# A selective-scan, attention and FFN kernel: two directions' state projection in one TensorE operation, attention sums from the rows' own product, GpSimd adds ahead of the means

## The chip, the cores and the metric

One core of a Trainium2 chip computes the whole batch in one launch. The metric is the device time of that launch in microseconds (us); lower is better. The engines are TensorE (PE in the profile, with its weight loads listed apart as PEld), VectorE (DVE), ScalarE (ACT), GpSimd (POOL) and SyncE (SP). SP issues the DMAs of this kernel, in order.

## What is computed

The input is 8 images of 96 channels by 64 x 64 pixels (4096 positions), in float32. Layer 0 adds a state-space block to the image, layer 1 adds linear attention and then a quantised FFN:

```python
x = x + ssm(group_norm(x))
t = tokens(x)                            # (8, 4096, 96)
t = t + attn(layer_norm(t)); t = t + ffn(layer_norm(t))

def ssm(x):
    xi, z = split(layer_norm(x) @ in_proj_w.T + in_proj_b)      # 192 channels each
    xi = silu(depthwise_conv3x3(xi) + conv_b)
    xs = 4 directions: rows, columns, and both reversed         # k = 0, 1, 2, 3
    dts, Bs, Cs = split(x_proj_w[k] @ xs[k], [6, 16, 16])       # the state projection
    delta = softplus(dt_proj_w[k] @ dts + dt_proj_b)
    h = exp(delta * A) * h + delta * u * Bs;  y = sum_n(h * Cs) + D * u   # scan, 4096 steps
    y = sum of the four directions, turned back to rows
    return (layer_norm(y) * silu(z)) @ out_proj_w.T + out_proj_b

def attn(x):                             # no softmax: linear in the sums of k and v
    q, k, v = split(x @ Wqkv + bqkv)     # 6 heads of 16
    return ((q @ k.T) * 16**-0.5 @ v) @ Wff + bff     # per head
```

## The kernel before

Images go in pairs; four pairs. The program is nine stages in a row: an opening stage that prepares pair 0, then scan of pair 0, then a mixed stage that finishes pair 0 and prepares pair 1, scan of pair 1, and so on; after the fourth scan a last stage only finishes pair 3. Four scans, three mixed stages, an opening and a last stage. Between the stages all operands pass through DRAM tensors: zs (gate), us (scan input), dl (the step sizes, split in three bf16 parts), du (step size times input), bs and cs (states), ys (scan results), t1 and tn (tokens before and after normalisation).

A scan (function `scan`) is written out in order, by hand. The other stages are not: each operation is handed to a planner, class `Plan`, with an engine, a cost in us, what it reads and writes, the buffers that it takes from a ring, and a rank. `Plan.run` then plays the stage forward by those costs and emits the operations in the order in which they would start. Of the operations of an engine that could start within 0.1 us of the earliest, the one of lowest rank goes first; a DMA is costed by its size at 0.23 MB/us. That order is fixed when the program is built, and each engine and SP work through theirs strictly in turn. An operation whose index is in `claims` and which lacks buffers keeps operations of worse rank from taking buffers of that ring. A `unit` ring ("unit", "set", "turn", "chunk") limits how many groups of operations are in flight.

What the stages consist of, with the ranks that order them (constants at the top of the file):

- `project`: group norm, layer norm and input projection, chunk by chunk (512 positions, 8 chunks, 2 images); ranks up to FRONT.
- `convolve`: nine taps, on DVE for two thirds of the channels (L540) and as 32 x 32 matmuls for the rest (L552), in two halves; ranks FRONT to CONV.
- `prepare`: for o = 0 (rows, k = 0 and 2) and o = 1 (columns, k = 1 and 3), for each chunk c: `states` (L637), the state projection, per direction k; an ACT copy of its bank `pt` to `S`; DMAs of B and C; `steps_` (L657), six small matmuls that make the step sizes; then per third T of the channels softplus, products and splits on ACT and DVE (L670, L682, L686), and stores of du and dl. For o = 1 POOL first turns u (L624). Ranks PREP (0.08) to 1. The channels of two images lie in three tiles of 128 partitions: image 0, image 1, and 64 + 64 remaining ones. `xw` holds the projection's weights, three slabs per direction.
- `back`: for each of 16 blocks (chunk and image): loads of yk (from ys), ut, z3, xr; yd adds on DVE and POOL (L984); transposes on PE that gather the directions (L998); the skip term (L1010); the mean over 192 channels as two accumulating matmuls (`both`, L1017, with the matrix j192), its subtraction (L1022), squares on ACT, their mean by `both` again, Ln and Exp for the root (`root`), norm and gate (L1030, L1033), output projection (`both` with woT), residual (L1038) and layer norm (`norm`, L407 to L415). Then attention: `keys` (L1050) multiplies the tokens by the weights of K and V, 128 tokens at a time, ACT copies to `kv`, and `outer` (L1057) sums K^T V over all tokens in a bank `pm` of its own. Ranks 0 to BACK. At the end K^T V becomes one 97 x 96 matrix per image, hm (L1070 to L1079).
- `tail`: for the 16 blocks again, once hm is there: tn and t1 loads, tokens times hm (L1107), residual, norm, the FFN in fp8 (L1115 to L1132), the last add on POOL (L1134) and the store. Ranks TAIL to TAIL_END.

PSUM has a ring `q` of five banks, which nearly all matmuls share, a ring `hold`, and pm. Every activation goes through line 296, every planned DMA through line 315.

## Time and profile before

| | us |
|---|---|
| median of 3 runs (10145.36 to 10156.27) | 10145.48 |
| profiled execution | 10155.55 |
| its span, first to last instruction | 10153.8 |
| opening stage, 0 to 529 | 529.1 |
| scans | 1781.0, 1782.6, 1780.8, 1777.9 |
| mixed stages | 717.9, 719.1, 719.6 |
| last stage | 345.8 |

Stage bounds are the first scan instruction on DVE (L855) of each scan and the end of its last. Over the span DVE is busy 90%, POOL 74%, PE and DMA's main queue 71% and 78%, ACT 69%; the granted TensorE clock is 0.88 on average. A share over the span mixes scans with the other stages, so a stage is read by itself, from windows. In a window PE busy counts the matmuls (weight loads overlap them and stand apart), DMA share is that of the core's 16 DMA engines, and it can exceed 1.

### The profile page before, as it was taken

What the parts mean: (1) busy time and instruction counts of PE and PEld (TensorE: products, weight loads), DVE (VectorE), ACT (ScalarE), POOL (GpSimd) and SP (SyncE); (2) the same over time, 40 slices, a digit from 0 to 9 for tenths busy, and PEclk for the clock granted to TensorE, in tenths of its full rate; (3) what the DMA queues carried; (4) which work ended last, traced back from release to release, by engine and by line L of the source; (5) the groups of instructions that cost most, each with busy time, mean ns of one, the idle gap of its engine ahead of it and who ended that gap; (6) DMA issues with size and microseconds to landing.
All of it is one profiled execution on the core that took longest, in us unless ns stands there. A gap on an engine that the chain in (4) does not pass through costs nothing. (4 is left out here: it accounts for less than half of the span.)

```text
span 10153.8 us, 382989 instructions
## 1 busy us (share of the span) xinstructions
PE 7238.0 (71%) x166080; PEld 5184.5 (51%) x166080; DVE 9133.4 (90%) x7072; ACT 7028.9 (69%) x12289; POOL 7542.1 (74%) x2416
## 2 busy tenths in 40 slices
PE   6666676667876667666886666666688666676678
PEld 2155565554425556555442555555543355565554
DVE  7699999997679999999778999999877899999985
ACT  5667777776777777776677777777667777777754
POOL 2099999991039999999104999999810599999971
PEclk7689989998878998988887999998888799988989
DMA  4988888886988888887698888878769788788884
GB/s 132 235 211 215 214 215 213 214 213 138 241 216 213 214 214 216 213 214 188 165 243 211 211 215 213 217 212 214 191 167 240 208 213 216 212 216 214 213 193 102
DMA packets 1593915, 2085.10 MB, mean 205 GB/s; under 512 B 409891, under 2 KB 1050404, under 8 KB 1588644
## 3 DMA queue, kind: packets, MB, share of 16 engines
q1 hardware_dynamic: 1592228, 2060.59, 78.3%
q8 instruction: 1304, 21.36, 1.0%
q14 instruction: 383, 3.14, 0.1%
HBM read 1601.99 MB, written 458.04 MB: 203 GB/s over the span
## 5 line engine op out<-in xcount | busy, mean ns | idle before, releaser
L855 DVE TENSOR_TENSOR_SCAN h<-da,dbu 128x774 f32<-128x774 f32 x4096 | 7025.9, 1759 | 139.5 <-POOL dbu L819 43.5
L819 POOL TENSOR_TENSOR dbu<-dut,bc 128x1536 f32<-128x1536 f32 x2048 | 7083.4, 3575 | 73.6 <-DMA dm<-dl 30.2
L844 ACT ACTIVATE da<-da 128x768 f32<-128x768 f32 x4092 | 3260.2, 797 | 1984.4 <-PE da L837 1968.0
L837 PE MATMUL da<-dm,aw 128*128 128x128 bf16 x24576 | 2279.9, 235 | 2268.3 <-DVE h L855 2078.8
L837 PEld LDWEIGHTS <-aw 128*128 128x128 bf16 x24576 | 1792.8, 104 | 2512.4 <-issue 2233.3
L873 PE MATMUL yp<-h,cw 128*32 128x48 f32 x131072 | 2904.7, 238 | 101.7 <-issue 88.3
L873 PEld LDWEIGHTS yp<-h,cw 128*32 128x32 f32 x131072 | 2412.1, 154 | 548.4 <-issue 228.3
L773 ACT ACTIVATE cw<-bc,blk 128x512 f32<-128x512 f32 x2048 | 1472.4, 720 | 74.3 <-DMA dut<-du 36.0
L984 POOL TENSOR_TENSOR yd<-yk 128x768 f32<-128x768 f32 x64 | 126.7, 1981 | 918.3 <-DMA yk<-ys 630.4
L1134 POOL TENSOR_TENSOR yk<-yk,yd 96x512 f32<-96x512 f32 x64 | 100.1, 1565 | 775.7 <-issue 406.0
L624 POOL COPY A<-A 128x512 f32<-128x512 f32 x96 | 135.7, 1423 | 676.6 <-ACT A L296 375.2
L881 ACT ACTIVATE yev<-yp 128x384 f32<-128x384 f32 x1024 | 505.4, 494 | 81.6 <-PE yp L873 81.3
L296 ACT ACTIVATE A<-A 128x512 bf16<-128x512 bf16 (+1 forms) x777 | 445.8, 618 | 145.1 <-DMA dl<-A 108.6
L816 ACT COPY dbu<-h 128x12 f32<-128x12 f32 x1984 | 409.2, 206 | 0.0
L682 DVE TENSOR_TENSOR A<-A 128x512 f32<-128x512 f32 x384 | 287.2, 751 | 88.6 <-ACT A L296 87.2
L657 PE MATMUL q<-A 6*64 6x512 f32 x1536 | 301.0, 734 | 78.7 <-ACT A L296 65.5
L686 DVE TENSOR_TENSOR A<-A 128x512 bf16<-128x512 f32 x384 | 279.8, 729 | 83.8 <-DMA dl<-A 81.6
L540 DVE SCALAR_TENSOR_TENSOR A<-A,c_convw,A 128x2048 f32<-128x2048 f32 x128 | 299.2, 2363 | 0.6
L998 PEld LDWEIGHTS q<-ident,yd 128*96 128x96 f32 x2048 | 248.1, 169 | 82.9 <-issue 62.2
L998 PE MATMUL q<-ident,yd 128*96 128x128 f32 x2048 | 260.9, 281 | 15.4 <-DVE yd L984 9.3
L296 ACT ACTIVATE A<-q,c_dtb 128x512 f32<-128x512 f32 x384 | 253.7, 677 | 7.0 <-PE q L657 6.0
L411 PE MATMUL q<-small,c_j 96*96 96x512 f32 x384 | 230.1, 693 | 28.8 <-ACT small L296 19.1
(125 smaller groups left out, 5271.8 us busy)
## 6 DMA issues: line engine op xcount, KB each, us to landing
dut<-du SPq DMA_DIRECT2D x2048, 384.0 KB
dm<-dl SPq DMA_DIRECT2D x1024, 288.0 KB
dl<-A SPq DMA_DIRECT2D x256, 384.0 KB
dm<-dl SPq DMA_DIRECT2D x1024, 96.0 KB
ys<-yev SPq DMA_DIRECT2D x1024, 96.0 KB
du<-A SPq DMA_DIRECT2D x256, 256.0 KB
bc<-cs SPq DMA_DIRECT2D x512, 128.0 KB
bc<-bs SPq DMA_DIRECT2D x512, 128.0 KB
```

What stands on the lines that cost most here:

```text
L296: "ACT", cost, lambda: nc.scalar.activation(dst(), src_(), func, **kw),
L540: dve(P, 2.34, lambda o=o, v=v, w=w: nc.vector.scalar_tensor_tensor(o, v, w, o, ALU.mult, ALU.add), (), wr, (), first + (CONV - FRONT) / 2 ...
L657: nc.tensor.matmul(P[pqs[T]][o : o + 64], dtw[at : at + RK, k, o : o + 64], P[S][at : at + RK], start=True, stop=True,)
L773: nc.scalar.activation(cw[i % 2][:, :, :, m, :].rearrange("p z j t -> p (z j) t"), bc[i][:, 1].rearrange("p z (j t) -> p (z j) t", j=NB), ...
L816: nc.scalar.copy(start, segs(hs[s - 1][:, :, r])[:, :, :, 1 if back else TC])
L819: nc.gpsimd.tensor_tensor(segs(t)[:, :, :, 1:], dut[g].unsqueeze(1) .to_broadcast([128, 2, NI, TC]), bc[s // NB][:, 0, :, bass.ts(c % NB, ...
L837: nc.tensor.matmul(e[:, i], aw[k, r][:, i, z, :], dm[s // 2][:, NI * r + i, bass.ts(c % 2, TC)], start=True, stop=True,)
L844: nc.scalar.activation(e, e, AF.Exp)
L855: nc.vector.tensor_tensor_scan(hs[s][:, w, r][:, d], da[p % 3][:, o : o + W6][:, d], dbu[4 * s + r][:, w][:, d], 0.0, ALU.mult, ALU.add,)
L873: nc.tensor.matmul(y[32 * q : 32 * q + 32, 2 * NE * i : 2 * NE * i + 2 * NE] .rearrange("p (j r i) -> p i j r", j=2, r=NR), w[:, z, :, t], ...
L881: nc.scalar.activation(yev[s][:, :, o : o + 8, :].rearrange("p j i e -> p i j e"), y[:, 0 : 16 * NE].rearrange("p (i j e) -> p i j e", j=2 ...
L998: nc.tensor.matmul(o, P[yd][:, k, j, DIM * g : DIM * g + DIM], ident, start=(k + j == 0), stop=(k + j == 4),)
```

## The change

The five ranks at the top change: projection and convolution take later ranks, the back blocks earlier ones, the tail ranks behind all of `prepare`.

`states` becomes one operation for the two directions k = o and k = o + 2. For k >= 2 the halves of image 0 and image 1 are swapped (`xw`, `S`, `dtw` and the DMAs of B and C follow), so that the products of the third tile, which are cut from 128 rows (half of them zeros) to the 64 rows that matter, are four 64 x 64 tiles in four quarters of the array. It takes two q banks at once and claims them. S becomes three deep; dtw is loaded in eight pieces instead of four.

Ahead of each of the two means POOL adds the two halves of 96 channels into a buffer of the ring `small` (now six deep in mixed stages), and the mean is one matmul.

`keys` gives way to `rows`: a transpose of the tokens (with the identity, 97 columns with the constant 1), one ACT copy of four blocks, and `outer` sums the 97 x 97 product of the tokens with themselves. After the last block that matrix is multiplied by the weights of K and of V, two more matmuls and copies per image.

```diff
-FRONT = 0.05
-CONV = 0.35
+FRONT = 0.2
+CONV = 0.5
-BACK = 0.7
-TAIL = 0.66
-TAIL_END = 1.29
+BACK = 0.39
+TAIL = 1.04
+TAIL_END = 1.25
...
-                    o = 64 * b + 32 * g
+                    o = 64 * (b ^ (k // 2)) + 32 * g
...
-            dma(P, 0.03, lambda at=at, o=o, n=n: dtw[at : at + RK, :, o : o + n],
-                lambda r=r, T=T, o=o, n=n: a["dtw"][:, r : r + RK, T, o : o + n].rearrange("k r c -> r k c"),
-                (), (f"dtw{at}",), (), -1)
-        ring(P, tmp, "S", 2, [128, F])
+            for k in (0, 2):
+                dma(P, 0.02, lambda at=at ^ 32 * k, k=k, o=o, n=n: dtw[at : at + RK, k : k + 2, o : o + n],
+                    lambda r=r, T=T, k=k, o=o, n=n: a["dtw"][k : k + 2, r : r + RK, T, o : o + n]
+                    .rearrange("k r c -> r k c"), (), (f"dtw{at}.{k}",), (), -1)
+        ring(P, tmp, "S", 3, [128, F])
...
+                pts = [f"pt.{k}.{c}" for k in (o, o + 2)]
+                def states(pts, o, u):
+                    for pt, k in zip(pts, (o, o + 2)):
+                        for b in range(2):
+                            h = slice(64 * (b ^ (k // 2)), 64 * (b ^ (k // 2)) + 64)
+                            nc.tensor.matmul(P[pt][h], xw[:, k, b, h], u[b](), start=True, stop=False)
+                    for pt, k in zip(pts, (o, o + 2)):
+                        for b in range(2):
+                            h = slice(64 * (b ^ (k // 2)), 64 * (b ^ (k // 2)) + 64)
+                            r = slice(64 * b, 64 * b + 64)
+                            nc.tensor.matmul(P[pt][h], xw[r, k, 2, h], u[2]()[r], start=False, stop=True)
+                P.unit = f"set.{o}.{c}"
+                P.claims.add(len(P.ops))
+                mm(P, 4.2, lambda pts=pts, o=o, u=u, states=states: states(pts, o, u),
+                   (*un[0], *un[1], *un[2], "xw"), pts, [(pt, "q") for pt in pts], rank)
                 for k in (o, o + 2):
                     n = f".{k}.{c}"
                     pt, S = "pt" + n, "S" + n
-
-                    def states(pt, k, u):
-                        for last in (False, True):
-                            for b in range(2):
-                                h = slice(64 * b, 64 * b + 64)
-                                nc.tensor.matmul(
-                                    P[pt][h], xw[:, k, 2 if last else b, h], u[2 if last else b](),
-                                    start=not last, stop=last,
-                                )
-
-                    P.unit = f"set.{k}.{c}"
-                    mm(P, 2.85, lambda pt=pt, k=k, u=u, states=states: states(pt, k, u),
-                       (*un[0], *un[1], *un[2], "xw"), (pt,), ((pt, "q"),), rank)
+                    P.unit = f"set.{o}.{c}"
...
-                                lambda S=S, r=r, b=b: P[S][64 * b + r : 64 * b + r + NS].rearrange(
+                                lambda S=S, r=r, h=64 * (b ^ (k // 2)): P[S][h + r : h + r + NS].rearrange(
                                     "p (j t) -> p j t", j=2), (S,), (), (), rank)
...
+                            at ^= 32 * (k & 2)
...
-        ring(P, tmp, "kv", 2, [128, 2, 2, DIM])
+        ring(P, tmp, "kv", 2, [128, 4, DIM + 1])
         P.ring("unit", [None] * 3)
-        pm = psm.tile([128, 2, DIM], F32, name="pm")
+        pm = psm.tile([128, 2, DIM + 1], F32, name="pm")
...
-            mm(P, 2.0, lambda mean=mean, yt=yt, both=both: both(mean, yt, lambda g: j192),
-               (f"{yt}#0", f"{yt}#1"), (mean,), ((mean, "q"),), rank)
+            def add(to, src_):
+                P.add("POOL", 1.25, lambda: nc.gpsimd.tensor_tensor(
+                    P[to], P[src_][:, 0], P[src_][:, 1], ALU.add),
+                    (f"{src_}#0", f"{src_}#1"), (to,), ((to, "small"),), rank)
+            def one(dst, src_):
+                mm(P, 1.03, lambda: nc.tensor.matmul(P[dst][:DIM], j192, P[src_], start=True, stop=True),
+                   (src_,), (dst,), ((dst, "q"),), rank)
+            sy, sv = "sy" + n, "sv" + n
+            add(sy, yt)
+            one(mean, sy)
...
-            mm(P, 2.0, lambda yv=yv, g_=g_, both=both: both(yv, g_, lambda g: j192),
-               (f"{g_}#0", f"{g_}#1"), (yv,), ((yv, "q"),), rank)
+            add(sv, g_)
+            one(yv, sv)
...
-            for h in range(2):
-                pk, kv = f"pk{h}" + n, f"kv{h}" + n
-
-                def keys(pk, to, h):
-                    for j in range(2):
-                        nc.tensor.matmul(
-                            P[pk][:, j * 2 * DIM : (j + 1) * 2 * DIM],
-                            P[to][:, bass.ts(2 * h + j, 128)], wkv, start=True, stop=True,
-                        )
-
-                def outer(kv, b, i, h):
-                    for j in range(2):
-                        nc.tensor.matmul(
-                            pm[:DIM, b], P[kv][:, j, 1], P[kv][:, j, 0],
-                            start=(i + h + j == 0), stop=(i == nblk // 2 - 1 and h + j == 2),
-                        )
-
-                mm(P, 0.86, lambda pk=pk, to=to, h=h, keys=keys: keys(pk, to, h), (to,), (pk,), ((pk, "q"),), rank)
-                act(P, lambda kv=kv: P[kv].rearrange("p j s e -> p (j s e)"), lambda pk=pk: P[pk][:, : 4 * DIM],
-                    AF.Copy, 0.49, (pk,), (kv,), ((kv, "kv"),), rank)
-                mm(P, 0.45, lambda kv=kv, b=b, i=i, h=h, outer=outer: outer(kv, b, i, h), (kv,), ("pm",), (), rank)
+            pk, kv = "pk" + n, "kv" + n
+            def rows(pk, to):
+                for j in range(4):
+                    nc.tensor.matmul(
+                        P[pk][:, j * (DIM + 1) : (j + 1) * (DIM + 1)], P[to][:, bass.ts(j, 128)],
+                        ident[0 : DIM + 1, 0 : DIM + 1], start=True, stop=True,
+                    )
+            def outer(kv, b, i):
+                for j in range(4):
+                    nc.tensor.matmul(
+                        pm[: DIM + 1, b], P[kv][:, j], P[kv][:, j],
+                        start=(i + j == 0), stop=(i == nblk // 2 - 1 and j == 3),
+                    )
+            mm(P, 1.0, lambda pk=pk, to=to, rows=rows: rows(pk, to), (to,), (pk,), ((pk, "q"),), rank)
+            act(P, lambda kv=kv: P[kv].rearrange("p j e -> p (j e)"), lambda pk=pk: P[pk][:, : 4 * DIM + 4],
+                AF.Copy, 0.49, (pk,), (kv,), ((kv, "kv"),), rank)
+            mm(P, 0.95, lambda kv=kv, b=b, i=i, outer=outer: outer(kv, b, i), (kv,), ("pm",), (), rank)
...
-            pg, ph = f"pg.{b}", f"ph.{b}"
-            dve(P, 0.2, lambda b=b, mt=mt: nc.vector.tensor_tensor(mt, pm[:DIM, b], hmask, ALU.mult),
-                ("pm",), (f"mt{b}",), (), BACK)
+            pg, ph, pa, pv = (f"{n}.{b}" for n in ("pg", "ph", "pa", "pv"))
+            gr, gk = (tmp.tile([DIM + 1, DIM + 1], F32, name=f"{n}{b}") for n in ("gr", "gk"))
+            dve(P, 0.2, lambda b=b, gr=gr: nc.vector.tensor_copy(gr, pm[: DIM + 1, b]), ("pm",), (f"gr{b}",), (), BACK)
+            mm(P, 0.3, lambda pa=pa, gr=gr: nc.tensor.matmul(
+                P[pa][: DIM + 1, :DIM], gr, wkv[:, 0:DIM], start=True, stop=True), (f"gr{b}",), (pa,), ((pa, "q"),), BACK)
+            dve(P, 0.2, lambda gk=gk, pa=pa: nc.vector.tensor_copy(gk[:, 0:DIM], P[pa][: DIM + 1, :DIM]), (pa,),
+                (f"gk{b}",), (), BACK)
+            mm(P, 0.3, lambda pv=pv, gk=gk: nc.tensor.matmul(
+                P[pv][:DIM, :DIM], wkv[:, DIM:], gk[:, 0:DIM], start=True, stop=True), (f"gk{b}",), (pv,),
+                ((pv, "q"),), BACK)
+            dve(P, 0.2, lambda pv=pv, mt=mt: nc.vector.tensor_tensor(mt, P[pv][:DIM, :DIM], hmask, ALU.mult),
+                (pv,), (f"mt{b}",), (), BACK)
...
-            ring(P, tmp, "small", 5 if old else 10, [DIM, F])
+            ring(P, tmp, "small", 6 if old else 10, [DIM, F])
```

More of the change, by code (lines that the diff above doesn't have):

```diff
@@ L662, in prepare @@
                     mm(P, 2.1, lambda pqs=pqs, k=k, S=S, steps_=steps_: steps_(pqs, k, S),
-                       (S, *[f"dtw{at}" for at, *_ in places]), pqs, [(q, "q") for q in pqs], rank)
+                       (S, *[f"dtw{at}.{k & 2}" for at, *_ in places]), pqs, [(q, "q") for q in pqs], rank)
                     P.unit = None
```

## The prediction

> **What bounds the kernel now.** I read the windows by stage first, then windows inside a stage, then groups by shape, then the waits. The columns of a window are stretch, length, busy us (and instructions) of PE, weight loads, DVE, ACT, POOL, then granted clock, DMA share, GB/s.
>
> ```profile
> 0.00:529.10 529.10, 341.19 (x1402) 97.02 (x1403) 364.99 (x446) 309.16 (x509) 96.69 (x58) 0.68 0.68 185
> 529.10:2310.10 1781.00, 1217.12 (x38646) 1045.84 (x38645) 1756.38 (x1024) 1269.57 (x2277) 1767.92 (x525) 0.90 0.81 211
> 2310.10:3028.00 717.90, 578.35 (x2874) 246.99 (x2875) 515.61 (x735) 498.78 (x806) 105.78 (x76) 0.84 0.80 203
> 9808.00:10153.80 345.80, 299.72 (x1472) 166.61 (x1472) 192.55 (x328) 147.12 (x258) 56.09 (x34) 0.91 0.63 129
> ```
>
> The page's 90% for DVE comes from the scans (1756 of 1781 us). The diff touches no scan, so four scans, 7122 us, stay. What can move is the opening stage (529 us), three mixed stages (718, 719, 720 us) and the last one (346 us). In a mixed stage PE is busiest, at 81%, with DMA at 80%: two candidates, so I cut the stages up.
>
> ```profile
> 2340.00:2760.00 420.00, 368.45 (x1994) 185.49 (x1993) 295.70 (x358) 296.03 (x456) 40.29 (x22) 0.92 0.79 195
> 2760.00:2980.00 220.00, 184.06 (x573) 48.26 (x572) 176.84 (x301) 175.90 (x303) 47.29 (x30) 0.76 0.85 228
> 2420.00:2560.00 140.00, 114.53 (x898) 58.15 (x898) 116.54 (x96) 101.73 (x149) 12.95 (x8) 0.91 0.45 117
> 9820.00:10000.00 180.00, 170.29 (x847) 109.82 (x848) 105.85 (x146) 65.43 (x112) 29.46 (x16) 0.96 1.09 214
> 140.00:200.00 60.00, 42.74 (x612) 19.44 (x610) 57.45 (x31) 39.73 (x59) 0.00 (x0) 0.84 0.24 83
> 220.00:500.00 280.00, 197.74 (x576) 42.73 (x576) 193.16 (x283) 178.67 (x312) 25.39 (x20) 0.62 0.90 233
> ```
>
> For 420 us of a mixed stage PE is 88% busy, with DVE and ACT at 70%; inside it lies a valley of 140 us in which DMA is 0.45 used. In its last 220 us PE, DVE and ACT are all at 80 to 84%. The last stage's back half has PE at 95% and DMA at 1.09 together. The opening stage is a DVE stretch (convolution, 57 of 60 us) and then a DMA stretch (0.90, 233 GB/s).
>
> **The change part by part.** Groups of a mixed stage; the numbers after the bar are busy us and mean ns of one:
>
> ```profile
> L637 PE MATMUL q<-A 128*64 128x512 f32 x128 | 50.1, 899 | 8.0 <-ACT A L296 3.1 <-POOL A L624 2.6 <-ACT small L296 2.2
> L637 PE MATMUL q<-A,A 128*64 128x512 f32 x128 | 36.8, 705 | 2.1 <-ACT kv L296 1.2 <-ACT A L296 0.6 <-DVE ta L1038 0.4
> L1017 PE MATMUL q<-g,j 96*96 96x512 f32 x64 | 31.7, 618 | 5.2 <-ACT A L296 2.8 <-ACT g L296 1.4 <-ACT small L296 0.6
> L1017 PE MATMUL q<-yt,j 96*96 96x512 f32 x64 | 30.4, 598 | 2.8 <-ACT A L296 1.6 <-DVE yt L1010 1.2
> L1050 PE MATMUL q<-c_wkv,tns 97*128 97x192 f32 x128 | 29.2, 366 | 11.5 <-DVE tns L415 6.1 <-DVE yt L1010 2.9 <-DVE ta L1038 1.6
> L1057 PE MATMUL pm<-kv 128*96 128x96 f32 x128 | 18.9, 276 | 8.5 <-ACT kv L296 8.4
> L1134 POOL TENSOR_TENSOR yk<-yk,yd 96x512 f32<-96x512 f32 x16 | 28.9, 1806 | 216.3 <-issue 133.2 <-DVE yd L1132 70.3 <-DMA dl<-A 12.5
> L474 DVE TENSOR_SCALAR A<-A 96x512 f32<-96x512 f32 x16 | 8.2, 534 | 0.0
> ```
>
> *States.* 32 operations cost 50.1 + 36.8 = 86.9 us, 2.72 each: four matmuls, two column halves side by side, so two steps of 1.36. A pair of directions costs four steps now. The new operation needs two steps for the full-row products and one for four quarter tiles if those run together: 3 x 1.36 = 4.07 against 5.43, 16 times, -21.7 us of PE (-9.2 in the first direction pair, inside the full 420 us; -12.5 later). Do quarter tiles run together? The timeline of L657 shows six matmuls of 64 columns in four row groups at the price of one:
>
> ```profile
> 2710.74 1.10 PE L657 MATMUL q<-A 6*64 6x512 f32 x12
> ```
>
> Two of the six (rows from 32 and 96) write halves of one bank at once, as the quarter tiles will. The Trainium skill, page "TensorEngine Tiling (Array Packing)", section "Restrictions and Gotchas", says that different row tiles cannot access one PSUM bank at the same time. By that rule the quarter tiles take two steps, the -21.7 us are gone, and the sum ends at 10030 instead of 9997; mine goes by the row. The first direction's eviction starts a step later, the second's earlier: 0, hidden by the other pair in flight (two "set" places, S now three deep); uncovered it would be 16 x 1.36 = 22 us. An operation that needs two free banks holds up all that PE has queued behind it; I put this inside the bounds of the order below.
>
> *Means.* 32 pairs of matmuls, 30.4 + 31.7 = 62.1 us, become single ones: -31.0 us of PE. 32 POOL adds of 96x512 come in, at L1134's 1.81 us, 58 us on an engine with 106 us of work in 718. That hides them as work. As a link in the block's chain an add of 1.81 us replaces 0.97 us of PE: +0.84, twice in 16 blocks, 27 us at most, 0 if the three units in flight cover it; I take 5, since the next block's matmuls fill PE now.
>
> DVE pays too. L474, 534 ns above, took 2166 ns in the opening stage, beside POOL operations of 10.9 us:
>
> ```profile
> L474 DVE TENSOR_SCALAR A<-A 96x512 f32<-96x512 f32 x16 | 34.0, 2166 | 0.0
> ```
>
> So POOL work can stop DVE. Bounds: 0, and 32 x 1.81 = 58 us of DVE; with DVE idle for 28% of the stage I put none of it on the path, and keep 20 for the range. The Trainium skill, page "SBUF — State Buffer", section "Who interferes with whom", speaks against this part: a DVE instruction with two SBUF inputs and a GpSimd one that reads SBUF exclude each other. By that rule alone the upper end of 58 us would be the value, a mixed stage would lose 16 us, and the sum would be 10171.
>
> *Attention sums.* 64 products of 192 columns (29.2 us) become 64 of 97, nearest row L1057's 18.9 x 97/96 = 19.1: -10.1 of PE; the outer products grow from 96 to 97, +0.2. Sixteen evictions of 0.49 go: -7.8 us of ACT. Four more small steps stand between pm and hm, some 1.5 us; 0 in a mixed stage, where preparation covers them, and 3 exposed in the last, whose second half waits for hm.
>
> *Order.* FRONT and CONV put projection and convolution later, BACK puts the back blocks earlier, TAIL puts the second half behind preparation. Each block moves with its yk, ut, z3, xr loads and t1, tn stores on SP, past the dl and du stores there, and its POOL add yd past the u copies. It could fill the valley: (0.90 - 0.45) x 140 = 63 us of DMA time; or leave PE-heavy second halves at the end, which costs up to the last stage's 114 us of them less what is idle beside preparation. Bounds -63 and +40, value 0: I can't derive an order from the profile. The rings (small 6, S 3) only take waits away. Four extra dtw loads on SP are 2 us, hidden by the convolution.
>
> *Sums.* Mixed stage: in the full stretch -31.0 - 10.0 - 9.2 = -50.2 us of PE; at its 88% share -44; of the -12.5 later, where three engines are level, and of ACT's -7.8, -3; the chain +5: -42. Three: -126. Last stage: -(30.2 + 31.4)/2 - 7 = -38 of PE, but DMA is full beside it: 180 us at 214 GB/s could be 167 at the 230 of its best slice, -13; the drain behind the last load perhaps -2, hm +3: -12. Opening stage: states -25 of PE lie beside a DMA stretch, 0; but preparation now ranks ahead of the convolution's second half, so its stores may start within the 60 us at 0.24: between -40 and +10, value -10. Total -148. From the profiled execution's 10155.55 (span 10153.8 and 1.75 around it) that is 10007.5; the median of the runs lies 10.07 lower, so 9997.
>
> **The rivals.** *The valley fills:* DMA becomes the only floor. A mixed stage has 0.80 x 718 = 574 us of it; at 0.92 that is 624, and with some 28 until the scan's first operation 652: -66 each. With -30 in the opening stage (three quarters of its bound) and -16 in the last (its -13 and the drain, hm hidden), -244: 9901. For it: the valley. Against: three engines level at 80% later. *Only transfers bind:* PE's relief turns into waiting for DMA, since outside the valley (2580 to 2980) its share is 0.90; only -10 remains, 10135. *Quarter tiles take turns:* without the state gain a mixed stage keeps -42 + 8 + 3 = -31, total -115, 10030. *POOL becomes the wait (slower):* its queue is in order, and its yd add waits for yk loads.
>
> ```profile
> POOL yd L984 <- DMA yk<-ys: 172.5, 11, 33.6
> SPq L315 <- DVE g L1033: 38.1, 7, 23.2
> ```
>
> A half-sum queued behind such an add inherits the wait, its mean stops PE's queue, and z3's release late holds the next loads on SP. If 60 us of the 172.5 are exposed per mixed stage, that is 60 - 42 = +18 each; a third of the last stage's 112 us of such waits, less 12, is +25; with -10 in the opening stage +69: 10215. It decides once an add waits on average for 42/32 = 1.3 us. Against it: an order in which the half-sums stand ahead of the next yd avoids it.
>
> **How the numbers follow.** PE relief (9940 to 10080 about 9997) 0.49; valley fills 0.13; quarter tiles take turns 0.06; only transfers bind 0.08; POOL 0.24. Measurements here tell 0.2% (20 us) from no change: faster 0.68, same 0.08, slower 0.24. The likeliest case alone is 9940 to 10080. Eight in ten: from below the valley case, 9890, up to part of the POOL case, 10190.
>
> **What would show it.** Right: L637's group near 65 us a mixed stage, j matmuls near 31, mixed stages near 676 us, the last near 334, PE's share below 81%. Wrong: quarter tiles starting one after the other; POOL adds whose gap is ended by yk loads, and PE gaps ended by POOL; DVE groups with two inputs longer than now (L682's 781 ns); or a stretch of second halves after preparation with DMA below 0.3.

## The result: 0.24% slower, and the profile after

The changed kernel takes 10172.15 us (median of 20 runs, 10154.79 to 10183.86) against 10146.24 for the kernel before in the same runs: ratio 1.0024 [1.0018, 1.003]. The forecast was 9997, faster. The time lies inside the stated range (9890 to 10190), whose upper end took in part of the POOL rival; the sign was wrong.

The windows by stage of the changed kernel (columns as in the prediction): opening, first mixed stage, last stage, then the valley of the mixed stage.

```profile
0.00:547.30 547.30, 330.07 (x1402) 87.97 (x1403) 355.82 (x446) 307.91 (x509) 101.64 (x57) 0.64 0.67 179
2327.80:3047.60 719.80, 548.91 (x2818) 235.29 (x2819) 527.77 (x739) 488.96 (x789) 190.55 (x107) 0.79 0.80 203
9817.90:10164.30 346.40, 280.55 (x1416) 152.77 (x1416) 205.23 (x332) 139.69 (x242) 98.15 (x66) 0.89 0.62 129
2507.80:2627.80 120.00, 91.33 (x844) 47.30 (x842) 96.14 (x76) 73.11 (x109) 46.93 (x18) 0.86 0.50 130
```

The opening stage grew from 529.1 to 547.3 us. The mixed stages take 719.8, 718.7 and 720.7 (mean 719.7, before 718.9), the last 346.4 (345.8). PE is busy 549 us of a mixed stage instead of 578, at a granted clock of 0.79 instead of 0.84; DVE 528 instead of 516; POOL 191 instead of 106. The valley of the DMA (0.45 in 140 us) has moved and not filled: 0.50 in 120 us. The four scans, which no edit touches, sum to between 7100 and 7122 us in the profiled executions of all kernels here, so what follows goes by stage lengths, each from one profiled execution. The three mixed stages of one kernel differ by up to 11 us, and the opening stage by 3 us where its program is the same (529.1 us before, 532.2 and 532.5 in `attn_only` and `loads_light` below), so less than about 5 us in one stage is not read.

Groups by shape of the first mixed stage, changed kernel (busy us, mean ns of one, then idle time before them and its releasers); under them L411 of the kernel before, a wait of the changed kernel, and its adds L1028 once more with min/median/max ns:

```profile
L636 PE MATMUL q<-A,A 128*64 128x512 f32 x64 | 26.5, 978 | 3.6 <-ACT A L296 3.6
L636 PE MATMUL q<-A 128*64 128x512 f32 x64 | 23.7, 872 | 7.5 <-DVE yk L1135 6.4 <-ACT yd L296 0.6 <-ACT A L296 0.5
L641 PE MATMUL q<-A,A 64*64 64x512 f32 x64 | 10.1, 702 | 0.0
L641 PE MATMUL q<-A 64*64 64x512 f32 x64 | 8.9, 624 | 0.7 <-POOL A L625 0.7
L1033 PE MATMUL q<-small,j 96*96 96x512 f32 x64 | 39.6, 708 | 28.7 <-POOL small L1028 26.0 <-ACT A L296 2.7
L1028 POOL TENSOR_TENSOR small<-yt 96x512 f32<-96x512 f32 x16 | 44.0, 2750 | 166.7 <-DVE yt L1017 160.7 <-PE q L495 4.2 <-PE q L1033 1.8
L1028 POOL TENSOR_TENSOR small<-g 96x512 f32<-96x512 f32 x16 | 38.3, 2394 | 74.5 <-ACT g L296 58.3 <-PE q L483 12.0 <-DMA t<-ta 4.1
L1067 PE MATMUL q<-ident,tns 97*128 97x97 f32 x128 | 21.7, 323 | 13.2 <-DVE tns L415 12.4 <-ACT A L296 0.7
L1074 PE MATMUL pm<-kv 128*97 128x97 f32 x128 | 18.3, 299 | 2.6 <-ACT kv L296 2.6
L411 PE MATMUL q<-small,c_j 96*96 96x512 f32 x96 | 62.0, 740 | 30.0 <-ACT small L296 28.2 <-ACT A L296 1.8
```

```profile
L411 PE MATMUL q<-small,c_j 96*96 96x512 f32 x96 | 57.4, 688 | 5.8 <-ACT small L296 2.6 <-DVE yt L1010 2.1 <-ACT A L296 1.1
```

```profile
POOL yd L991 <- DMA yk<-ys: 24.6, 3, 22.4
L1028 POOL TENSOR_TENSOR small<-yt x16: 1261/2216/6440, 2367.9 to 2717.5; 96x512 f32<-96x512 f32 x16
L1028 POOL TENSOR_TENSOR small<-g x16: 1259/1267/10304, 2373.3 to 2726.7; 96x512 f32<-96x512 f32 x16
```

States (L636 and L641) now take 69.2 us instead of 86.9, means (L1033) 39.6 instead of 62.1, rows and outer products 40.0 instead of 48.1. Against that L411, which no edit touches, takes 740 ns for one instead of 688. The adds (L1028) take 2.75 and 2.39 us in the mean, not the 1.81 of the sum or the 1.25 of the planner, and PE waits 26.0 us for them. The mean hides two kinds: eleven of the 32 take 1.26 or 1.27 us, the planner's figure, and nine take 3.3 to 10.3 us, eight of these beside the convolution's taps on DVE (L540). The longest one starts within a run of taps and ends 1.1 us after the last of them (that one at 2587.74, for 2.34 us):

```profile
2580.08 6.87 DVE L540 SCALAR_TENSOR_TENSOR A<-A,c_convw,A 128x2048 f32<-128x2048 f32 x3
2580.91 10.30 POOL L1028 TENSOR_TENSOR small<-g 96x512 f32<-96x512 f32 x1 [5.40 <-ACT g L296]
```

DVE gets longer too: L540 takes 2569 ns in the mean instead of 2342, L474 886 instead of 534.

The timeline of one place in that stage (start, length in us, then what ran; in brackets the idle time before it and what ended it):

```profile
2617.19 3.31 SPq L315 DMA_DIRECT2D us<-A  x2
2624.24 7.14 SPq L315 DMA_DIRECT2D us<-A  x4
2625.21 1.94 PE L636 MATMUL q<-A,A 128*64 128x512 f32 x8
2627.08 1.09 PE L641 MATMUL q<-A,A 64*64 64x512 f32 x8
2633.50 4.31 SPq L315 DMA_DIRECT2D bs<-A  x2
2637.87 0.90 SPq L315 DMA_DIRECT2D cs<-A  x2
2641.97 0.60 ACT L296 ACTIVATE A<-q 128x512 f32<-128x512 f32 x1 [13.17 <-DMA cs<-A]
2643.10 2.02 PE L411 MATMUL q<-small,c_j 96*96 96x512 f32 x2 [12.01 <-ACT small L296]
2645.08 0.69 DVE L677 TENSOR_TENSOR A<-A,A 128x512 f32<-128x512 f32 x1 [21.80 <-ACT A L296]
```

Two things are seen. Four quarter tiles (eight matmuls, as an f32 product is listed as two) take 1.09 us where eight full-row ones take 1.94: they do run together. And SP spends 10 us on issuing six stores of `us`; the stores of B and C that free a buffer of the ring S come behind them; ACT's next copy into S waits 13.2 us, and behind ACT wait PE (12.0) and DVE (21.8). All engines stand still for 10.9, 11.6 and 11.9 us at this place, about 303 us into each mixed stage; before, the longest such stop of a mixed stage was 5.3 us, and one on this buffer 2.6.

The opening stage has a stop as well. All engines stand still for 9.3 us at 39 us, where ACT waits 12.1 us, until 48.65, for `inz`, a bias that the projection needs. In the first 500 us of the stage before, no such stop was over 3.3 us. It is not where the stage gets longer, though. The load of `inz` stands behind small stores of `ad` (weights made ready for the scans) in both kernels, 17 of them now and 19 before, and the same activation started at 50.31 us before, after a wait of 5.4 us. The convolution starts on DVE at 119.6 us now and at 119.0 before. The difference opens behind that, in PE's part of the convolution (L552, two blocks), which the first state projection (L637, now L636) follows. Before, then now:

```profile
179.05 12.03 PE L552 MATMUL q<-A,diag 32*32 32x512 f32 x282 [0.87 <-ACT A L296]
191.01 1.08 PE L637 MATMUL q<-A,A 128*64 128x512 f32 x4
```

```profile
190.64 11.25 PE L552 MATMUL q<-A,diag 32*32 32x512 f32 x282 [0.86 <-ACT A L296]
201.82 1.08 PE L636 MATMUL q<-A,A 128*64 128x512 f32 x4
```

Before, the last matmul of the input projection (159.34 us) stands ahead of the first block of taps. With the new FRONT and CONV three of them (173.57 to 179.2 us) stand between the two blocks and ACT evicts them before it empties the first block's banks; the bulk of the second block starts 11.6 us later, and the first state projection 10.8.

### The profile page after: what moved, and what is told of

Its sections match the earlier page's. It is cut to its first block, busy times and chain, and to the rows that moved or that the text cites. A ratio compares the mean times of both kernels' runs of the same rounds, so it can differ in the third digit from the quotient of the medians.

```text
span 10164.3 us, 382694 instructions
## 1 busy us (share of the span) xinstructions
PE 7120.0 (70%) x165856; PEld 5121.7 (50%) x165856; DVE 9172.2 (90%) x7088; ACT 6986.9 (69%) x12222; POOL 7840.0 (77%) x2544
## 5 line engine op out<-in xcount | busy, mean ns | idle before, releaser
L1028 POOL TENSOR_TENSOR small<-yt 96x512 f32<-96x512 f32 x64 | 152.4, 2381 | 570.7 <-DVE yt L1017 544.2
L1028 POOL TENSOR_TENSOR small<-g 96x512 f32<-96x512 f32 x64 | 135.4, 2115 | 283.0 <-ACT g L296 238.7
L540 DVE SCALAR_TENSOR_TENSOR A<-A,c_convw,A 128x2048 f32<-128x2048 f32 x128 | 319.7, 2524 | 0.4
L411 PE MATMUL q<-small,c_j 96*96 96x512 f32 x384 | 241.1, 724 | 101.3 <-ACT small L296 90.6
L1005 PEld LDWEIGHTS q<-ident,yd 128*96 128x96 f32 x2048 | 250.3, 172 | 110.4 <-issue 58.3
L689 DVE TENSOR_TENSOR A<-A 128x512 f32<-128x512 f32 x384 | 285.9, 748 | 13.9 <-ACT A L296 12.7
```

What stands on the lines that cost most here:

```text
L540: dve(P, 2.34, lambda o=o, v=v, w=w: nc.vector.scalar_tensor_tensor(o, v, w, o, ALU.mult, ALU.add), (), wr, (), first + (CONV - FRONT) / 2 ...
L1005: nc.tensor.matmul(o, P[yd][:, k, j, DIM * g : DIM * g + DIM], ident, start=(k + j == 0), stop=(k + j == 4),)
```

## The experiments

My theory after the result: taking work from PE is worth little here, and POOL's adds and the new order cost what little there was. The rival: PE's relief is worth what I said, and one new wait takes it all back. A stage is planned anew whenever an operation is added or its cost changes, so there are two kinds of runs: those in which an order is kept and an instruction only made lighter, and those in which parts are put in or taken out and the planner writes another order.

**What PE's relief is worth, order kept.** `pe_light` is the kernel before with 74 us of PE's work gone from each mixed stage: half of each mean and the third tile's product of the states.

```diff
-                        for last in (False, True):
+                        for last in (False,):
...
+                n = 1 if w(0) is j192 else 2
-                for g in range(2):
+                for g in range(n):
```

> The kernel before, in its own order (all planned costs kept), with PE work left out: each mean takes only the first half of the channels (one matmul for two), and the state projection leaves out the third tile. That is 31 + 43 = 74 us less PE work per mixed stage, 31 in the last, 43 in the opening one, more than the change takes out. Theory R (PE is not on the path): mixed stages within 10 us of 718 and a lower granted clock than 0.84. The prediction's theory (PE relief counts at 88% of the full stretch): mixed stages near 718 - 50 = 668, total about 9980.

10088.66 us, ratio 0.9945 [0.9922, 0.9968]. Mixed stages 714.5, 704.7, 704.3, mean 707.8: -11 us for 74, or 15%. The window of its second one:

```profile
4801.30:5506.00 704.70, 549.67 (x2682) 240.32 (x2683) 517.04 (x735) 498.87 (x806) 106.70 (x76) 0.79 0.80 207
```

PE is busy 550 us where 578 - 74 = 504 were to be expected: the granted clock is 0.79 here (0.76 to 0.79 in the three), 0.84 before, and what is left of PE's work takes longer. One by one: L411 takes 719, 733 and 740 ns in the three mixed stages, 688, 717 and 697 before. In the last stage, where PE is busiest by far and only the means' 31 us go, 15 us are saved (331.2).

**The quarter tiles alone, order kept.** `full_rows` is the changed kernel with the third tile's product over all 128 rows.

```diff
-  nc.tensor.matmul(P[pt][h], xw[r, k, 2, h], u[2]()[r], start=False, stop=True)
+  nc.tensor.matmul(P[pt][h], xw[:, k, 2, h], u[2](), start=False, stop=True)
```

> The changed kernel in its own order, with the third tile's products over all 128 rows again (half of the weights are zeros) in place of quarter tiles; the two directions stay in one operation, the result is the same. 16 x 2 x 0.43 us more of PE at full clock, some 15 to 20 us per mixed stage. Theory R (PE time is paid back by the granted clock): mixed stages within 4 us of 720, opening stage within 4 us of 547, and a higher granted clock. The prediction's theory (88% of PE time counts in the full stretch): mixed stages 8 us or more longer.

10164.36 us, 1.0025 [1.0016, 1.0035], the same as the changed kernel. Mixed stages +2.1 us in the mean, opening stage 547.0. The quarter tiles, though they run as meant, can't be seen in the time. The window of its opening stage shows where it goes: more work, at a clock of 0.68 instead of 0.64.

```profile
0.00:547.00 547.00, 331.49 (x1402) 93.97 (x1403) 356.69 (x447) 308.07 (x509) 101.92 (x57) 0.68 0.67 179
```

**The adds, order kept.** `adds_light`: each add covers 16 columns instead of 512, and the mean reads the first half, so that PE does the same work and does not wait for POOL. `adds_unwaited`: the same with the full adds.

```diff
-                    P[to], P[src_][:, 0], P[src_][:, 1], ALU.add),
+                    P[to][:, 0:16], P[src_][:, 0, 0:16], P[src_][:, 1, 0:16], ALU.add),
...
-  mm(P, 1.03, lambda: nc.tensor.matmul(P[dst][:DIM], j192, P[src_], start=True, stop=True),
+  mm(P, 1.03, lambda: nc.tensor.matmul(P[dst][:DIM], j192, P[half_src][:, 0], start=True, stop=True),
```

(`adds_unwaited` has the second hunk alone.)

> The changed kernel in its own order, with POOL adding only 16 of 512 columns and the means taken from the first half of the channels directly, so that no mean waits for POOL. Rival P (adds of 2.4 to 2.75 us in the chain and DVE slowed by them): mixed stages 15 to 40 us shorter than 720. Theory R: less than 8 us shorter.

> The changed kernel in its own order, with the POOL adds at full size but no mean waiting for them (each mean is taken from the first half of the channels). With adds of 16 columns and no wait the mixed stages were 699, with the change 720. If the price is the wait for POOL in the chain: 698 to 704. If it is DVE slowed by POOL's reads: 712 to 720.

`adds_light`: 10098.43 us, 0.9958 [0.9939, 0.9978]; mixed stages 699.4 in the mean (-20.3), last stage 335.4 (-11). `adds_unwaited`: 10126.87, 0.9986 [0.9976, 0.9996]; 709.6 (-10.1), last 342.1. A window of each, in this order:

```profile
2326.50:3024.40 697.90, 544.89 (x2818) 234.35 (x2819) 512.94 (x738) 488.45 (x789) 150.25 (x107) 0.79 0.81 209
```

```profile
2322.20:3028.90 706.70, 545.75 (x2818) 234.58 (x2819) 530.78 (x739) 488.50 (x789) 189.19 (x107) 0.79 0.80 206
```

So 32 adds cost at least 20 us of a mixed stage (the short ones still take 1.4 us in the mean): half as a link that PE waits for, half by their length on POOL. Where the second half lies is read from DVE's busy time: 531 us with the full adds that no mean waits for, 513 with the short ones. Of the instructions with two inputs in SBUF, L540 gets shorter (2597 to 2482 ns), and so does L677 where the two are different tiles (788 to 684); so does L474, with one (892 to 703). L1040, which takes one of its inputs from PSUM, takes 675 ns in both. The rival, that other work waits for POOL's queue, has little room: in the first mixed stage of `adds_unwaited` no wait of PE, ACT or DVE for POOL sums to over 2.2 us, and SP's waits for POOL sum to 37 us, 34 in `adds_light`.

**The wait for S, order kept.** `us_light`: the changed kernel with 7/8 of the bytes of the `us` stores left out; the back blocks load the gate `zs` in place of `us`.

```diff
+                hq_ = slice(h * L // 2, h * L // 2 + 256)
-                spread(P, 1.05, lambda o, n, hs_=hs_: us[o : o + n, hs_], T,
+                spread(P, 1.05, lambda o, n, hs_=hq_: us[o : o + n, hs_], T,
```

> The changed kernel in its own order, with seven eighths of the stores of the scan input (us) left out, 5.5 MB per mixed stage; the back blocks read the gate in its place. In the profile of the changed kernel ACT waits 13.2 us for the landing of a cs store that stands behind these stores, and all engines stand still with it. If that wait is on the path: mixed stages 10 to 20 us shorter; if it only moves waiting that comes later anyway: under 5.

10115.81 us, 0.9978 [0.9966, 0.9989]; mixed stages 712.2, 704.5, 709.2, mean 708.6: -11 us, and the stop at 303 us is gone from all three. That is the whole length of the stop, but a quarter of the 42 us that were missing: the rival, one wait that takes all back, falls. The 5.5 MB less in each stage are no likely cause: `loads_light` below leaves out 11 MB and gains 1.5 us.

**Ranks and parts apart, orders new.** `ranks_only` is the kernel before with the five new ranks. `parts_old_ranks` is the changed kernel with the five old ones. `states_only` and `attn_only` put one part of the change into the kernel before, old ranks. `no_adds` takes the adds out of the changed kernel and puts the paired matmuls back. `old_opening` gives the opening stage alone the old FRONT and CONV.

```diff
-            add(sy, yt)
-            one(mean, sy)
+            mm(P, 2.0, lambda mean=mean, yt=yt, both=both: both(mean, yt, lambda g: j192),
+               (f"{yt}#0", f"{yt}#1"), (mean,), ((mean, "q"),), rank)
...
+        FR, CO = (FRONT, CONV) if beside else (0.05, 0.35)
```

The first hunk is `no_adds` (the other mean likewise), the second `old_opening` (FR and CO then stand for FRONT and CONV in `project` and `convolve`). The other four take their lines from the diff of the change: `ranks_only` its first hunk, `parts_old_ranks` all but that one, `states_only` those of `xw`, `dtw`, S and `states`, `attn_only` those from the ring kv and pm on, without the adds.

> The kernel before with the five new ranks and nothing else. Theory R (ranks cost the opening stage, and the relief of PE is not on the path of a mixed stage): the opening stage goes from 529 to about 547 us, the mixed stages stay within 5 us of 718, total about 10165. Rival P (the POOL adds eat what ranks and relief bring): with the new ranks and no adds the mixed stages get shorter, by 10 us or more each, total below 10135.

> The changed kernel with the five old ranks. Theory R: opening stage back at about 529 us; mixed stages 718 within 8, last stage 346, total 10140 to 10160. Rival P: mixed stages longer than 725, since the adds stay and the order that made room for them is gone, total over 10165.

> The kernel before with the paired state projection (and S three deep, dtw in eight loads) and nothing else: old ranks, old attention, old means. With all parts and the old ranks the mixed stages were 768 and the opening stage 535. If the pairing, with two banks claimed at once, is what suffers under the old ranks: mixed stages 740 to 770. If the adds are: mixed stages 715 to 725. Opening stage 535 to 537 in both cases.

> The kernel before with the attention sums from the rows' own product and nothing else: old ranks, old states, old means. 10 us less of PE and 8 us less of ACT per mixed stage. If PE and ACT work counts at the 15% that PE work was worth when left out: mixed stages 715 to 719, total 10130 to 10140. Rival (the new order costs more than the work saved): mixed stages over 722.

> The changed kernel with both means as two matmuls again, without the POOL adds; its costs are in the planned order, so the order changes too. Theory R: mixed stages 718 to 728 us (31 us more of PE, hidden), total 10165 to 10200. Rival P: mixed stages 10 us or more shorter than 720, last stage shorter than 346, total below 10145.

> The changed kernel, with FRONT 0.05 and CONV 0.35 in the opening stage alone. Theory R: the opening stage falls from 547 to 529 +- 4 us and all other stages stay, total about 10150, level with the kernel before. Rival Q (the opening stage is longer because the paired state projection starts later): it stays above 540, total about 10170.

| | ratio to before | opening | mixed, mean of 3 | last |
|---|---|---|---|---|
| before | 1 | 529.1 | 718.9 | 345.9 |
| after | 1.0024 [1.0018, 1.003] | 547.3 | 719.7 | 346.4 |
| ranks_only | 1.0066 [1.0051, 1.0081] | 541.4 | 739.5 | 343.4 |
| parts_old_ranks | 1.0143 [1.0128, 1.0158] | 535.4 | 767.9 | 350.2 |
| states_only | 1.0061 [1.0047, 1.0075] | 534.2 | 741.0 | 345.8 |
| attn_only | 1.0022 [1.0013, 1.0031] | 532.2 | 725.4 | 347.0 |
| no_adds | 1.0015 [1.0005, 1.0024] | 547.3 | 718.5 | 346.6 |
| old_opening | 1.0010 [1.0001, 1.002] | 536.1 | 720.9 | 346.1 |

Nothing here adds up. The ranks alone cost 20.6 us a mixed stage, all the parts with the old ranks 49, the paired states alone 22, and ranks and parts together 0.8. The new ranks suit the new parts and not the old ones. Several expectations failed with this: both for `ranks_only`, and the first for `parts_old_ranks` and for `attn_only`, since I had taken a new order as nearly free. `old_opening` fell between its two. Taking the adds out and 31 us of PE back in lets some 15 us be expected by the runs at a kept order (20 less 15% of 31); with the order that the planner then writes, the 1 us that it gives can't be told from nothing. The stop at the ring S is still there in that order, 13 to 14 us at 290 to 295 us. An edit's own cost and the cost of the order that it brings about are of one size (`ranks_only` changes the order alone), and the second is not in any row of a profile.

The opening stage can be taken apart: its ranks are worth 11 to 12 us (541.4 against 529.1, and 547.3 against 536.1), paired states 5 to 7 against 529.1, or 2 to 4 against the 532 of the same program in other kernels (534.2, 535.4 and 536.1, all with the old ranks). The first lies ahead of the preparation, as in the timelines above: the first state projection starts at 190.3 to 193.4 us in `old_opening`, `states_only` and `attn_only`, at 202.8 in `ranks_only`. The stop at 39 us is in every kernel with the new FRONT there and in none with the old one (`ranks_only` 9.25 us), but the convolution starts at 118.4 to 121.1 us in all of those named here. The second lies in what follows: from the first state projection to the scan it is 338 to 339 us with the old projection (before, `ranks_only`, `attn_only`), 346 in `after` and `old_opening`, 341 in `states_only`. For it I have no cause that was tested: PE's clock is lower there (400 to 500 us: 0.55 after, 0.65 before), but `full_rows` raised the clock and left the length. With lighter `us` stores (`us_light`) it is 340.5 us; no run lightens them in the kernel before.

**What the stage hangs on.** Four lighter versions of the kernel before, order kept; `pe_light` above is one. `conv_light`: eight of DVE's nine taps on a quarter of the rows (first hunk). `no_tables`: no loads of activation tables on ACT, with Silu and Softplus replaced by Identity and Exp (second hunk, one of its lines). `loads_light`: 7/8 of the bytes of the yk loads of k = 2 and 3 left out, 11 MB, and k = 0 and 1 added to themselves (third hunk, one of its lines). `all_light`: all four.

```diff
-  o, v, w, o, ALU.mult, ALU.add), (), wr, (), first + (CONV - FRONT) / 2 * (9 * (T // 2) + t) / 18)
+  o[:, 0:8], v[:, 0:8], w, o[:, 0:8], ALU.mult, ALU.add), (), wr, (), first + (CONV - FRONT) / 2 * (9 * (T // 2) + t) / 18)
...
-  act(P, lambda d=d: P[d], lambda pq=pq: P[pq], AF.Softplus, 0.675, (pq, "w_dtb"), (d,),
+  act(P, lambda d=d: P[d], lambda pq=pq: P[pq], AF.Exp, 0.675, (pq, "w_dtb"), (d,),
...
+                    ns = 1 if k > 1 else 8
-                    dma(P, 0.4, lambda yk=yk, k=k: P[yk][:, k],
+                    dma(P, 0.4, lambda yk=yk, k=k, ns=ns: P[yk][:, k, 0:ns],
```

> The kernel before, in its own order, with eight of nine taps of the convolution on DVE over a quarter of the rows only; some 50 us less DVE work per mixed stage, all of it before preparation can begin. If DVE's convolution is what preparation waits for, and it sets the stage: mixed stages 25 to 50 us shorter than 719, opening stage 30 to 50 us shorter than 529. If the length is set by queues and waits later on: mixed stages under 12 us shorter.

> The kernel before, in its own order, with Silu and Softplus replaced by Identity and Exp, so that all functions of ACT lie in one table and none of the 54 table loads of a mixed stage (1.28 us each, 69 us of ACT) is made. If ACT sets the mixed stage: 30 to 65 us shorter than 719. If ACT is one of several at 70%: 5 to 20 us shorter.

> The kernel before, in its own order, with seven eighths of the scan results of directions 2 and 3 not loaded (directions 0 and 1 are added to themselves instead): 11 of 146 MB per mixed stage, of the smallest packets. If transfers bind a mixed stage where its DMA share is 0.9 and over: mixed stages 25 to 45 us shorter, last stage 40 us or more shorter. If the order and the waits between engines bind it: under 10 us per mixed stage, last stage at most 20.

> The kernel before, in its own order, with the work left out of pe_light, conv_light, loads_light and no_tables together: 74 us of PE, 50 of DVE, 69 of ACT, 11 MB of loads per mixed stage. Alone, the first three brought 11, 5 and 2 us. If the engines take turns in binding: much more than the sum, mixed stages under 650. If latencies and the fixed order of the queues set the length: about the sum of the parts, 718 minus 20 minus what no_tables brings.

| | taken out of a mixed stage | mixed, mean of 3 | worth | ratio |
|---|---|---|---|---|
| pe_light | 74 us of PE | 707.8 | -11 | 0.9945 [0.9922, 0.9968] |
| conv_light | 50 us of DVE | 713.5 | -5 | 0.9985 [0.9975, 0.9995] |
| no_tables | 71 us of ACT (54 table loads, 69 us) | 710.9 | -8 | 0.9961 [0.9947, 0.9975] |
| loads_light | 11 MB of DMA, share 0.80 to 0.71 | 717.5 | -1.5 | 0.9987 [0.9975, 0.9998] |
| all_light | all of it | 682.5 | -36 | 0.9851 [0.9823, 0.988] |

```profile
2292.00:2969.10 677.10, 540.77 (x2682) 234.71 (x2683) 462.95 (x735) 427.26 (x752) 104.50 (x76) 0.79 0.75 199
```

No one of the four is the bound: what is taken from an engine is worth 11 to 15% of its time, and the 48 us of transfer (11 MB at 230 GB/s) 3%, which can't be told from nothing. All four together give 36 us, ten more than the 26 of the parts. Five means with the scatter above don't settle whether that is more than the sum, so whether they take turns as the bound stays open. Even then, in the window above (`all_light`, first mixed stage), PE is busy 541 us at a clock of 0.79, DVE 463, ACT 427, and DMA's share is 0.75, in 677 us. What fills the rest are waits from engine to engine in queues that run in order; which of these chains sets the length I have not found.

**Versions meant to be better.** `us_later` stores `us` chunk by chunk behind the stores of B and C. `combo` joins it with the old ranks in the opening stage and the means without adds; `combo2` is `combo` with the old `us` stores in the opening stage.

```diff
-                spread(P, 1.05, lambda o, n, hs_=hs_: us[o : o + n, hs_], T,
...
+                for T in range(3 if o == 0 else 0):
+                    spread(P, 0.26, lambda o_, n_, cs=cs: us[o_ : o_ + n_, cs], T, lambda T=T, cs=cs: xi[T][:, cs],
+                           [*gated(T, c), *[f"bc.{k_}.{c}.{r}.{b}" for k_ in (0, 2) for r in (RK, 32 + RK) for b in range(2)]],
+                           (), rank)
```

> The changed kernel with the us stores cut into chunks, each put behind the B and C stores of its chunk, so that no burst of us stores stands ahead of the B and C stores that free S. Nothing is left out. The 11 to 12 us for which all engines stand still at ACT's copy to S should be gone: mixed stages 706 to 712 instead of 720, opening stage 541 to 545 instead of 547, total about 10135. Rival (the order made by the planner decides, and a new order is as likely worse): mixed stages 715 or more.

> The changed kernel with the three repairs at once: means as two matmuls without POOL adds, the old FRONT and CONV in the opening stage, us stores in chunks behind the B and C stores. If the gains add: opening stage 532 to 537, mixed stages 704 to 712, last stage 346, total 10095 to 10125, ahead of both kernels. Rival (the order decides): mixed stages 715 or more, total 10140 or more.

> As combo (means as two matmuls, the old FRONT and CONV in the opening stage, us stores in chunks), but the us stores in chunks in the mixed stages alone. In combo and in us_later the opening stage was 10 to 12 us longer with chunked us stores, the mixed stages 4 to 7 us shorter. If the parts add: opening stage 534 to 538, mixed stages 710 to 714, last stage 345, total 10112 to 10125. Rival (the order decides): opening stage over 542 or mixed stages over 716.

`us_later`: 10171.33 us, 1.0029 [1.0018, 1.004]; mixed stages 715.3, opening 557.2: the stop at 303 us is gone from all three mixed stages, but of `us_light`'s 11 us a stage 4 are got, and 10 are lost in the opening. `combo`: 10130.72, 0.9993 [0.9984, 1.0002]; mixed 712.1, opening 548.1. `combo2`: 10122.92, 0.9983 [0.9974, 0.9992]; opening 534.3, mixed 710.4, 712.8, 716.7, last 342.4. It beats both kernels: 0.17% under the one before, about 0.4% under the changed one.

In its first mixed stage (710.4 us) PE is busy longer than in the changed kernel (563 us), DVE and POOL less (509 and 121); the stage is 9 us shorter, and the mean of the three (713.3) 6.

## Why the prediction was wrong

Its instruction counts held, its durations in part. Three steps for a pair of directions: 65.2 us by the sum (16 x 4.07), 69.2 measured, and 65.2 x 0.84/0.79 = 69.3 is the same at the clock that was granted. Quarter tiles take the time of one; the rule of the Trainium skill, page "TensorEngine Tiling (Array Packing)", section "Restrictions and Gotchas", that different row tiles cannot access one PSUM bank at a time, is not seen here (1.09 us for all four, halves of a bank from different row tiles). Attention's sums cost PE 8 us less, and ACT is busy 10 us less. The means gave 22.5 us instead of 31: a single matmul takes 708 ns, one of a pair took 598 and 618, which is more than the clock accounts for.

These steps failed:

- *"At its 88% share -44".* PE's busy share was taken for the share of its relief that reaches the end. `pe_light` gives 15% of 74 us; by that share the 63 us of the sum are worth about 9. Two reasons, both seen there: no engine is the bound, so relief becomes idle time on PE; and part of it never becomes idle time, since the granted clock falls (0.84 to 0.79) and the remaining matmuls get longer (L411 688 to 717 ns before, 719 to 740 in `pe_light`). The Trainium skill, page "TensorE: Matmul & The Clock Gate", Part 1, says that the clock is set by how busy PE has been lately; the windows agree in direction, and the prediction left it out.
- *The adds: "I take 5" for the chain and 0 for DVE.* 20 us a mixed stage, 10 for the wait and 10 for their length, which DVE's busy time shows, and 11 in the last. The rival on POOL named the mechanism only in part: PE's gaps are ended by POOL (26.0 us), but POOL's own gaps before an add are mostly ended by DVE and ACT (160.7 and 58.3 us), and waits of yd for yk loads fell from 172.5 to 24.6 us. What was mis-sized was an add beside the convolution's taps, 3.3 to 10.3 us instead of 1.81 (elsewhere many take 1.26), and DVE beside it. The Trainium skill, page "SBUF — State Buffer", section "Who interferes with whom", spoke for this, and DVE's 513 against 531 us agree; it was weighed and priced at 0 on the path because DVE was idle for 28% of the stage. That the prediction's sum by this page's rule, 10171, lies beside the 10172 measured is luck: it put 58 us of DVE on the path, where 10 were found, and kept the -44 of PE. Of the signs named, L682's group (now L689) did not lengthen (771 ns after 781); L540 and L474 did. Idle shares hide nothing if the instruction that is slowed is the next in a chain.
- *Order: "bounds -63 and +40, value 0".* The orders measured lie within it, and its middle meant nothing. The ranks cost the old parts 20.6 us a mixed stage, the old ranks cost the new parts 48, and the order of the changed kernel put six stores ahead of those that free S, 11 us. The step "the rings (small 6, S 3) only take waits away" was wrong for S: a third buffer doesn't help when the stores that free all of them are queued behind others.
- *Opening -10: +18.2.* Preparation was to start earlier, since it ranks ahead of the convolution's second half. It starts 10.8 us later (201.8 us, 191.0 before): PE's second block of taps stands ahead of it in both kernels, and with the new FRONT and CONV the last projection chunk stands ahead of that block. The rest, some 7 us, came with the paired states and has no tested cause. *Last stage -12: +0.5.* PE's relief counts there (`pe_light` -15), and the adds took 11 of it; the some 5 us still missing are open.

By stage, +18.2 + 3 x 0.8 + 0.5 make +21.1, of the 26 us between the medians. The two profiled executions differ by only 10.5 us (10164.3 - 10153.8), because the scans, which no edit touches, sum to 7122 us in the one of the kernel before, more than in any other here, and to 7111 in the changed kernel's. For a mixed stage the pieces at a kept order, -9 for PE, +20 for the adds and +11 for S, would make +22 if they added up, which no run shows, and +0.8 was measured. The 21 us between stay open: the new order would have to be better by so much elsewhere.

## What to carry to other kernels

Measure the worth of an engine's relief before buying it: make its instructions lighter at the same order and look at the stage, for relief of an engine that was busy 81% of a stage, and 88% of its fullest stretch, was worth 15% here. Where a planner fixes the order, an edit brings a new order whose cost can be as large as the edit's own, so compare edits with the order kept, and look in the new trace for places where all engines stand still. Then check that such a stop lasts: the one in the opening stage was made good before the convolution began. An operation moved to an idle engine isn't free if it stands in the chain of the busy ones, or if it and another engine's instructions lengthen each other.

## What the hardware showed that was not expected

- PE's granted clock follows its load here even in a stage where it is busy three quarters of the time: 0.84 at 578 us of 718, 0.79 with 74 us of work less, 0.76 in the 771 us stage of `parts_old_ranks` (582 us busy). Work taken away comes back in part as longer matmuls.
- One POOL add of two 96 x 512 f32 halves takes 1.26 us where DVE is idle beside it (2619.43 in the timeline of the changed kernel, DVE between two instructions), and up to 10.3 us beside the convolution's taps on DVE, whose inputs both lie in SBUF. With 16 columns (`adds_light`) the shortest takes 0.22 us and the mean still 1.4 (L1028: 1384 and 1402 ns), so most of a short add's time is not its data.
- 69 us of ACT's time in a mixed stage went into 54 table loads of 1.28 us, and taking them away was worth 8.
